# A message-passing layer on one core: fewer PSUM banks for the gather tiles, hand-written orders on four engines, and the next pair's products moved between the tiles

## The chip, the core and the metric

The kernel runs on one core of a Trainium2 chip. A core has five engines that run side by side and wait for each other by semaphores: TensorE (PE; its weight loads are PEld in the profile), VectorE (DVE), ScalarE (ACT), GpSimd (POOL) and SyncE (SP, which here only loads registers and issues transfers). [...] The metric is the device time of one execution in microseconds. Three runs of the kernel before gave 5231.43, 5231.67 and 5264.13, with a median of 5231.67.

## The reference

There are 12500 nodes with 32 features and 400000 edges, sorted by their destination. Every edge takes the normalised features of its source and its destination and 32 features of its own through two small layers. Every node takes the maximum over the edges that end in it.

```python
h = jnp.maximum(_layernorm(x, axis=-1), 0.0)
e_feat = jnp.concatenate([h[src], h[dst], edge_attr], axis=-1)   # 96 features
hid = jax.nn.relu(e_feat @ W1 + b1)                              # 64
v = hid @ W2 + b2                                                # 32
x_cand = jax.ops.segment_max(v, dst, num_segments=num_nodes)
out = x + jnp.maximum(x_cand, h)
```

## The kernel before, in words

The edges are cut into four stripes (`NS`), which lie side by side on the partitions, 32 features each. Every stripe is worked through in 196 chunks (`NCH`) of 512 edges, so that a chunk holds 2048 edges. The main loop takes two chunks, a pair, per turn: 98 turns. The first layer is split in three products that are added up in the PSUM tiles `ph0` to `ph3`, one for each stripe:

- the edge's own features: weights `w1c`, moving data `ea`, a plain transfer;
- the destination: since edges are sorted, a stripe's chunk ends in a window (span) of at most 32 nodes. The window's rows of a table `q` are the weights (`qw`), and a one-hot `of` (which node of the window an edge ends in) is the moving data. DVE makes `of` by comparing the destination numbers `db` with the node numbers `node` (line 370);
- the source: rows of `h` gathered by GpSimd with indirect DMAs of 128 rows (`gather`, line 143), turned into features by edges with a DVE transpose (`to_features`, lines 324 and 326).

Most chunks have 16 groups of 128 source rows. GpSimd gathers 12 of them, and TensorE fetches the last four (`MM`) by matmul, which the code calls tiles: a one-hot `hot` of the group of 14 nodes, in seven parts and two halves of `h` (14 matmuls, line 295), picks all features of the group, a matmul with `its` (line 292) puts a large negative number on the 13 wrong nodes, and DVE's maximum over the 14 (line 297) leaves the right row in `gm`. `hot` and `its` are made by DVE (lines 285 and 287). A pair has eight such tiles. They prepare the pair that follows; the four tiles of a chunk are taken by `next(tiles, None)` at given places of the loop.

After ACT's relu (`hid`, line 389) the second layer goes to `pv` (line 399). A DVE scan (line 404) runs the maximum along the edges, starting again at every new destination by the penalties `pb`. `leave_1` transposes the scan's result by TensorE (line 336) and adds the bias (`so`, line 338); DVE makes a one-hot `last` of the edges that are the last of their node (line 340). `leave_2` multiplies the two (line 350), ACT copies the result (`wo`, line 353), and SP writes the four windows to DRAM (line 357).

PSUM is used as follows: `ph0` to `ph3` one bank each, `pv` three buffers that tiles and second layers take in turn, `tr` one for both `leave` steps. The buffers of gathered rows are six, so the gathers of a pair can start when the transposes of the pair three turns ahead have read theirs; they are 24 in a row.

The order on SP and PE is that of the program (`manual_schedule(engines={SP, PE})`). On DVE and ACT a scheduler sets it: it puts the two transposes of line 324 for the next pair right after the product that reads the present pair's `ht`. So in DVE's stream they stand one pair ahead of their place in the program.

## Time and profile before

| | |
|---|---|
| median of 3 runs | 5231.67 us |
| profiled execution | 5227.3 us |
| its span | 5225.5 us |
| mean granted TensorE clock | 0.810 |
| PE busy | 3638.2 us (70%) |
| DVE busy | 1846.3 us (35%) |
| POOL busy | 2238.9 us (43%) |
| ACT busy | 315.6 us (6%) |
| HBM traffic | 48 GB/s over the span |

The profile is that of one execution. A row of its groups gives the line, the engine, the operation, what it writes and reads, and how often; then the busy time and the mean duration of one in ns; then how long the engine stood idle just before such instructions and what ended the wait ("issue": nothing that the profile shows; "remote": a signal whose sender had long ended). In the slices, each digit is a fortieth of the span in tenths. In a timeline, a row is a start, a time, an engine, a line and an operation, with how many were merged (x14), and in brackets how long the engine was idle before it. The first 163 us prepare tables; the loop over pairs takes the rest, but for the last some 25 us.

### The profile page before, as it was taken

What the parts mean: (1) busy time and instruction counts of PE and PEld (TensorE: products, weight loads), DVE (VectorE), ACT (ScalarE), POOL (GpSimd) and SP (SyncE); (2) the same over time, 40 slices, a digit from 0 to 9 for tenths busy, and PEclk for the clock granted to TensorE, in tenths of its full rate; (3) what the DMA queues carried; (4) which work ended last, traced back from release to release, by engine and by line L of the source; (5) the groups of instructions that cost most, each with busy time, mean ns of one, the idle gap of its engine ahead of it and who ended that gap; (6) DMA issues with size and microseconds to landing.
All of it is one profiled execution on the core that took longest, in us unless ns stands there. A gap on an engine that the chain in (4) does not pass through costs nothing. (4 is left out here: it accounts for less than half of the span.)

```text
span 5225.5 us, 57318 instructions
## 1 busy us (share of the span) xinstructions
PE 3638.2 (70%) x20281; PEld 2775.9 (53%) x20281; DVE 1846.3 (35%) x3612; ACT 315.6 (6%) x627; POOL 2238.9 (43%) x2369
## 2 busy tenths in 40 slices
PE   2376767676767676767676767676767676777687
PEld 1255555555555555555554555555555555555565
DVE  2333333333333333333333333333333333333344
ACT  1000000000000000000000000000000000000000
POOL 6534344444444444444444444444444444444420
PEclk6587878787878787878788888787878787878788
DMA  3321112211211121112111211121112211211121
GB/s 123 90 58 43 42 39 58 44 41 40 58 42 41 40 56 44 40 40 56 44 40 40 57 44 40 40 56 44 41 40 57 44 41 40 57 44 40 40 53 65
DMA packets 235577, 256.47 MB, mean 49 GB/s; under 512 B 123653, under 2 KB 211861, under 8 KB 222102
## 3 DMA queue, kind: packets, MB, share of 16 engines
q10 hardware_dynamic: 74084, 137.60, 9.7%
q0 software_dynamic: 75296, 38.70, 5.6%
q1 hardware_dynamic: 85906, 76.48, 4.9%
q8 instruction: 159, 2.61, 0.2%
q14 instruction: 132, 1.08, 0.1%
HBM read 238.44 MB, written 14.04 MB: 48 GB/s over the span
## 5 line engine op out<-in xcount | busy, mean ns | idle before, releaser
L143 POOL DMA_INDIRECT gh<-h_d,src_i x2353 | 2234.8, 950 | 2812.1 <-DVE ht L324 2098.3
L295 PE MATMUL pv<-hs,hot 128*128 128x448 f32 x10808 | 2874.0, 413 | 712.6 <-issue 712.4
L295 PEld LDWEIGHTS pv<-hs,hot 128*128 128x128 f32 x10808 | 2282.8, 212 | 1444.9 <-issue 1270.9
L297 DVE TENSOR_REDUCE gm<-pv 128x32 f32<-128x448 f32 x772 | 481.2, 623 | 2548.3 <-remote 1529.4
L292 PE MATMUL pv<-others,its 128*128 128x448 bf16 x772 | 301.9, 391 | 427.0 <-issue 386.0
L285 DVE TENSOR_SCALAR hot<-kb,key_p 128x512 fp32r<-128x512 f16 x1351 | 555.8, 479 | 9.5 <-DMA qw<-q_d 9.5
L350 PE MATMUL tr<-so,last 128*128 128x128 f32 x1568 | 250.2, 282 | 250.0 <-issue 240.8
L404 DVE TENSOR_TENSOR_SCAN sm<-pb,sm,pv 128x512 f32<-128x512 bf16 x195 | 248.9, 1276 | 469.3 <-remote 332.5
L350 PEld LDWEIGHTS tr<-so,last 128*128 128x128 f32 x1568 | 227.1, 197 | 229.5 <-issue 211.8
L389 ACT ACTIVATE hid<-ph,wt 128x512 f32<-128x512 f32 x392 | 239.3, 690 | 973.5 <-PE ph L379 529.9
L292 PEld LDWEIGHTS <-its 128*128 128x128 bf16 x772 | 78.0, 101 | 400.5 <-issue 387.4
L353 ACT ACTIVATE wo<-tr 128x128 f32<-128x128 f32 x196 | 54.5, 278 | 3810.7 <-remote 1817.6
L336 PE MATMUL tr<-ident,sm 128*128 128x128 f32 x784 | 146.0, 319 | 22.3 <-ACT wo L353 22.3
L336 PEld LDWEIGHTS tr<-ident,sm 128*128 128x128 f32 x784 | 117.9, 167 | 57.9 <-ACT wo L353 38.4
L338 DVE TENSOR_TENSOR so<-tr,wt 128x512 f32<-128x512 f32 x196 | 133.9, 683 | 24.1 <-PE pv L292 11.5
L340 DVE TENSOR_TENSOR last<-iota_w,at 128x512 f32<-128x512 f32 x196 | 131.6, 672 | 28.2 <-PE tr L350 28.2
L324 DVE STREAM_TRANSPOSE ht<-gh 128x384 f32<-128x384 f32 (+1 forms) x196 | 102.9, 563 | 71.0 <-PE ph L379 54.8
L379 PE MATMUL ph<-ea,wt 32*64 32x512 f32 x1568 | 110.0, 617 | 8.4 <-DMA ea<-in_edge_attr 8.4
L379 PE MATMUL ph<-ht,wt 32*64 32x512 f32 x1568 | 110.9, 612 | 0.5 <-issue 0.4
L379 PE MATMUL ph<-of,qw 32*64 32x512 f32 x1568 | 105.5, 592 | 6.2 <-issue 6.2
L399 PE MATMUL pv<-hid,wt 64*32 64x512 f32 x1568 | 108.9, 604 | 0.2 <-ACT hid L389 0.2
L287 DVE TENSOR_SCALAR its<-kb,place 128x512 bf16<-128x512 f16 x193 | 69.6, 361 | 96.4 <-remote 80.1
(68 smaller groups left out, 399.3 us busy)
## 6 DMA issues: line engine op xcount, KB each, us to landing
ea<-in_edge_attr SPq DMA_DIRECT2D x49, 1024.0 KB
db<-in_dst_ext ACTq DMA_DIRECT2D x196, 256.0 KB
kb<-key_d ACTq DMA_DIRECT2D x193, 256.0 KB
gh<-h_d,src_i POOLq DMA_INDIRECT x2353
pb<-pen_d ACTq DMA_DIRECT2D x196, 128.0 KB
qw<-q_d SPq DMA_DIRECT2D x784, 8.0 KB
top_d<-wo SPq DMA_DIRECT2D x784, 4.0 KB
top_d<-zero ACTq DMA_DIRECT2D x2, 1568.0 KB
```

Source lines behind the costliest of these rows:

```text
L143: nc.gpsimd.indirect_dma_start(out=gh[:, k, :], out_offset=None, in_=h_d[:, :], in_offset=bass.IndirectOffsetOnAxis(ap=src_i[:, c, k:k + 1 ...
L285: nc.vector.tensor_scalar(hot[:, k], kb[:, 0], key_p[:, k:k + 1], None, op0=ALU.is_equal)
L292: nc.tensor.matmul(po, its[:, e], others.rearrange("p f a -> p (f a)"), start=True, stop=False)
L295: nc.tensor.matmul(po, hot[:, k, e], hs[:, part, k].rearrange("p f a -> p (f a)"), start=False, stop=(k == A1 - 1 and part == 1))
L297: nc.vector.tensor_reduce(gm[:, m, :], po.rearrange("p (f a) -> p f a", a=A0), axis=AX.X, op=ALU.max)
L336: nc.tensor.transpose(px[:, j, :], sm[:, j * P:(j + 1) * P], ident)
L338: nc.vector.tensor_tensor(so, px, b2r[:, None, :].to_broadcast([P, J, P]), op=ALU.add)
L340: nc.vector.tensor_tensor(last, iota_w[:, None, None, :].to_broadcast([P, J, NS, W]), at[:, :, c * J:(c + 1) * J].rearrange("p s j -> p j ...
L350: nc.tensor.matmul(pw, last[:, j].rearrange("p s w -> p (s w)"), so[:, j, :], start=(j == 0), stop=(j == J - 1))
L379: nc.tensor.matmul(ph[s][x * HID:(x + 1) * HID], w[g], e[g], start=start, stop=stop)
L389: nc.scalar.activation(hid[s], ph[s], AF.Relu, bias=b1c)
L404: nc.vector.tensor_tensor_scan(sm, loaded.pop(c + x)[2], pv[x], before, op0=ALU.add, op1=ALU.max)
```

## The change

- **PSUM.** `pv` has two buffers instead of three. The free bank holds `iota_ps`, a copy of the constants 0 to 31 that `last` is compared with; before, they were read from SBUF.
- **One-hots of node spans.** ACT makes `of` with two activations: relu(1 - (db - node)^2). The constants are kept with the other sign (`below`).
- **Orders.** DVE and ACT are in program order too. Each turn of the loop names the place of every operation. The transposes are done at the start of the pair that needs them.
- **Interleaving.** The products of the next pair's edge features and windows into `ph` are done in this turn, after the third tile and after the second layer. The window sums of a pair's second chunk (`leave_2`) are done in the turn that follows.
- **Window sums.** `leave_2` computes two blocks of 64 by 64 instead of one of 128 by 128, of which it had read only the diagonal; ACT copies half the columns.
- **Loads.** `AHEAD` is 4 chunks instead of 2; `db` and `pb` are one transfer each for all stripes; `kb` is loaded for two chunks at once; SP loads the window starts for a pair at once, from a transposed table, without bounds checks; `qw` has eight buffers, `sm` and `of` three.

```diff
-AHEAD = 2
+AHEAD = 4
...
-            tc.manual_schedule(engines={SP, PE}):
+            tc.manual_schedule(engines={SP, PE, DVE, ACT}):
...
+        iota_ps = ps.tile([P, C], F32, name="iota_ps")[:, :W]
+        nc.vector.tensor_copy(iota_ps, iota_w)
...
+        def tile(c, m):
...
+            hot, its = hots[c]
+            e = slice(m * P, (m + 1) * P)
+            po = ps.tile([P, C], F32, name="pv", bufs=2)[:, :D * A0]
+            nc.tensor.matmul(po, its[:, e], others.rearrange("p f a -> p (f a)"), start=True, stop=False)
+            for k in range(A1):
+                for part in range(2):
+                    nc.tensor.matmul(po, hot[:, k, e], hs[:, part, k].rearrange("p f a -> p (f a)"),
+                                     start=False, stop=(k == A1 - 1 and part == 1))
+            rows = mm_rows[c][:, m, :]
+            nc.vector.tensor_reduce(rows, po.rearrange("p (f a) -> p f a", a=A0), axis=AX.X, op=ALU.max)
...
-                for s in range(NS):
-                    g = slice(s * D, (s + 1) * D)
-                    nc.scalar.dma_start(db[g, :n], ap(dst_ext, 1 + s * S + c * C, [[0, D], [1, n]]))
-                    nc.scalar.dma_start(pb[g, :n], ap(pen_d, s * S + c * C, [[0, D], [1, n]]))
+                nc.scalar.dma_start(db[:, :n], ap(dst_ext, 1 + c * C, [[S, NS], [0, D], [1, n]]))
+                nc.scalar.dma_start(pb[:, :n], ap(pen_d, c * C, [[S, NS], [0, D], [1, n]]))
...
+        def window_hots(c):
+
+            of = ofs[c] = pool.tile([P, C], F32, name="of", bufs=3)
+            nc.scalar.activation(of, loaded[c][1], AF.Square, bias=below[:, c:c + 1])
+            nc.scalar.activation(of, of, AF.Relu, bias=ones, scale=-1.0)
...
-                nc.tensor.matmul(pw, last[:, j].rearrange("p s w -> p (s w)"), so[:, j, :],
-                                 start=(j == 0), stop=(j == J - 1))
+                for g in range(2):
+                    nc.tensor.matmul(pw[g * 2 * W:(g + 1) * 2 * W],
+                                     last[:, j, 2 * g:2 * g + 2].rearrange("p s w -> p (s w)"),
+                                     so[:, j, g * 2 * D:(g + 1) * 2 * D], start=(j == 0), stop=(j == J - 1))
...
+            a, b = c + 2, c + 3
+            gh = [gather(c + x) for x in range(2)]
+            load_keys(a + 2)
             for k in range(c + AHEAD, min(c + AHEAD + 2, NCH)):
                 load(k)
...
             ht = [to_features(c + x, gh[x]) for x in range(2)]
-            into_ph([(w1a, ht[x]) for x in range(2)], False, True)
+            into_ph(ph, [(w1a, ht[x]) for x in range(2)], False, True)
             hid = []
             for s in range(NS):
                 hid.append(pool.tile([P, C], F32, name="hid", bufs=6))
                 nc.scalar.activation(hid[s], ph[s], AF.Relu, bias=b1c)
...
+            for k in range(a, min(a + 2, NCH)):
+                window_hots(k)
+            tile(a, 0)
+            one_hots(b, range(3))
+            tile(a, 1)
+            one_hots(b, range(3, A1))
+            last = [lasts(c)]
+            tile(a, 2)
+            ph = edges_into(a)
+            pv = [ps.tile([P, C], F32, name="pv", bufs=2) for x in range(2)]
             for s in range(NS):
                 for x in range(2):
                     g = slice(x * HID, (x + 1) * HID)
                     nc.tensor.matmul(pv[x][s * D:(s + 1) * D], w2x[g], hid[s][g], start=True, stop=True)
+            windows_into(a, ph)
+            leave()
             sms = []
...
+            tile(a, 3)
+            so = leave_1(c, sms[0])
+            last.append(lasts(c + 1))
+            tile(b, 0)
+            one_hots(a + 2, range(4))
+            leave_2(c, so, last[0])
+            tile(b, 1)
+            so = leave_1(c + 1, sms[1])
+            one_hots(a + 2, range(4, A1))
+            tile(b, 2)
+            tile(b, 3)
+            leave = lambda c=c + 1, so=so, last=last[1]: leave_2(c, so, last)
+        leave()
```

In the order that follows from it, TensorE's turn is: the product of `ht`; tiles a0, a1, a2; the edges' product of the next pair; the second layer; the windows' product of the next pair; the window sums of the last turn's second chunk; tile a3; transposes of the first chunk; tile b0; window sums of the first chunk; tile b1; transposes of the second chunk; tiles b2 and b3. DVE's turn is: four transposes (rows of the gathers and of the tiles, by turns); the maxima of a0 and a1 with one-hots between them; `last`; the maximum of a2; two scans; the maximum of a3; and so on to the maxima of b2 and b3.

## The prediction

> **What bounds the kernel.** I read the page's slices first, then its groups, then stretches with and without gathers, then one pair in order of time. A pair is two chunks, one turn of the loop.

> ```profile
> PE   2376767676767676767676767676767676777687
> PEclk6587878787878787878788888787878787878788
> ...
> L143 POOL DMA_INDIRECT gh<-h_d,src_i x2353 | 2234.8, 950 | 2812.1 <-DVE ht L324 2098.3
> ...
> L297 DVE TENSOR_REDUCE gm<-pv 128x32 f32<-128x448 f32 x772 | 481.2, 623 | 2548.3 <-remote 1529.4
> ...
> L353 ACT ACTIVATE wo<-tr 128x128 f32<-128x128 f32 x196 | 54.5, 278 | 3810.7 <-remote 1817.6
> ```

> TensorE is busy some 70% of every slice, at a granted clock of about 0.8. DVE and ACT stand idle for "remote": the awaited signal came, but nothing that had just ended explains the moment.

> ```profile
> 2502.50:2555.30 52.80, 37.88 (x213) 28.96 (x213) 20.22 (x41) 2.98 (x6) 22.71 (x24) 0.82 0.10 20
> ...
> 5073.35:5104.75 31.40, 31.40 (x210) 25.55 (x210) 18.22 (x37) 3.23 (x7) 0.00 (x0) 1.00 0.18 42
> ```

> The columns are the stretch, its length, busy us (instructions) of PE, PEld, DVE, ACT and POOL, clock, DMA share, GB/s. The second row is a pair at the end, when all gathers are issued: TensorE is never idle, at full clock, and the pair takes 31.2 us. With 24 gathers in it the same pair takes 52.8 (from gather burst to burst 52.2 on average). So a burst of gathers costs 21 us a pair. The timeline shows how:

> ```profile
> 2521.50 0.95 POOL L143 DMA_INDIRECT gh<-h_d,src_i  x1 [23.02 <-DVE ht L324]
> ...
> 2527.01 1.09 PE L399 MATMUL pv<-hid,wt 64*32 64x512 f32 x16
> ...
> 2528.07 3.13 PE L295 MATMUL pv<-hs,hot 128*128 128x448 f32 x14
> ...
> 2531.50 1.28 DVE L404 TENSOR_TENSOR_SCAN sm<-pb,sm,pv 128x512 f32<-128x512 bf16 x1 [3.60 <-PE pv L295]
> ...
> 2533.62 0.35 DVE L287 TENSOR_SCALAR its<-kb,place 128x512 bf16<-128x512 f16 x1 [0.84 <-remote]
> ...
> 2544.13 0.53 PE L295 MATMUL pv<-hs,hot 128*128 128x448 f32 x1 [1.57 <-issue]
> 2546.23 0.53 PE L295 MATMUL pv<-hs,hot 128*128 128x448 f32 x1 [1.57 <-issue]
> ...
> 2550.28 0.95 POOL L143 DMA_INDIRECT gh<-h_d,src_i  x1 [0.30 <-issue]
> ...
> 2553.24 0.62 DVE L297 TENSOR_REDUCE gm<-pv 128x32 f32<-128x448 f32 x1 [18.08 <-remote]
> ...
> 2555.33 0.91 PE L295 MATMUL pv<-hs,hot 128*128 128x448 f32 x2 [0.87 <-issue]
> ```

> Call the first gather G (2521.50). The product that the scan needs ends at 2528.1; the scan starts at 2531.50. The tile begun at 2528.04 is computed by 2531.2, but its maximum starts at 2553.24. Between the signal for `its` (a tile's first weights) and that for the tile's end lie 28 TensorE instructions (14 weight loads, 14 matmuls): 19.6 us, 0.70 each. So in a burst TensorE's completions reach the others one per 0.70 us, small matmul or large. The scan's signal is roughly the 81st instruction after G and comes at G+10.0, so some 66 pass freely (81 - 10.0/0.70). TensorE runs about 65 instructions ahead of what has been told, then crawls itself, 0.70 or 1.40 apart. It ends at G+33.8 (2555.33), 5 us after the last gather's start. I know no cause, only the pace; DVE and ACT instructions that don't wait for TensorE run promptly.

> **The change, part by part.** TensorE's work, from this timeline: a tile 3.01 us (30 instructions), each of three groups into `ph` 1.05 (32), the second layer 1.03 (32), transposes of a chunk 0.52 (8), window sums 0.97 (16). 8 x 3.01 + 3 x 1.05 + 1.03 + 2 x 0.52 + 2 x 0.97 = 31.2, the pair without gathers. Before, 17.0 of that lies between the end of the slow stretch and the next G (2502.5 to 2521.5, which took 19.0: the clock was at half at first, so 1.9 is lost), and 14.2 is done in the 33.8 us from G.

> *Hand order of DVE.* The transposes of gathered rows, which release the next burst, stood a pair ahead in DVE's stream; now they stand after the maximum of the pair's last tile, and TensorE's next instruction after that tile is the product that reads them. Nothing covers this: 0.1 signal + 0.62 maximum + four transposes (rows 563 and 304 ns, about 1.6 as they overlap) + 0.1 = 2.4 us of idle TensorE a pair. G falls after the first, 1.6 after the tile, 0.85 before the product. Below zero is excluded: before, no such wait stands in the trace.

> *TensorE order with two tile banks.* From G: product of `ht` (32 instructions), tiles a0, a1, a2 (90), products of the next pair's edges (32), then the second layer into both banks that a1 and a2 hold. It waits for DVE's maximum of a2, and that for a2's end, instruction 122 after G. At one per 0.70 us it is told at (122 - 66) x 0.70 = 39 us, later than the stretch's end; so at G+33.8 all is told, the maximum takes 0.62 and the second layer starts at G+34.6. Until then TensorE has done 1.05 + 9.03 + 1.05 = 11.1 us of work, not 14.2. Behind the waiting matmul are queued the window products, the previous chunk's window sums (for which ACT's copy, then SP's writes wait) and tile a3; behind DVE's waiting maximum, both scans.

> [...] By the rows 3.01 against 0.62 two banks do outside the burst: cost 0. [...]

> *One-hots of node spans on ACT.* Two fewer DVE operations (482 ns), four more activations (690 ns), 2.8 us. They run under a0 to a2 (9 us) and are needed after the second layer. DVE has 18 us of work in 52. Cost 0; uncovered it would be 2.8 on TensorE.

> *Constants in PSUM.* `last` costs 672 ns; the PSUM-reading `so` 683: nothing. [...] By the row it is 0: POOL's idle time before a gather is 0.30 with DVE busy or not, and in the worst stretch DVE did nothing for 18 us. I take 0.

> *Window sums.* Eight products 64x64 for four 128x128, so 32 instructions for 16. Nearest row 0.11 us per weight load; between 0.5 (halves side by side) and 1.8 (every instruction at the old price); I take 0.9, as half the columns load per instruction. They stand after the stretch. Ends: -80 and +175 us over 196.

> *Loads.* ACT issues two `db`/`pb` transfers for eight, one `kb` for two; SP reads registers once a pair, without bounds steps; loads run a pair further ahead, past SP's writes. These queues wait for `wo` most of the time (3382.9 us on SP); cost 0, hidden by a pair's lead (over 50 us).

> Sum of a pair: 33.8 + 0.8 + (31.1 - 11.1 = 20.0) + 1.9 half clock + 1.6 to the next G = 58.1, against 52.2: +5.9. About 94 pairs carry a burst, four don't (+2.4 each): 555 + 10 = +565 on the profiled execution's 5227.3 (span 5225.5), which is 0.1% under the median of 5231.67. Forecast 5795.

> **The rivals.**
> *The second layer gets in early* (chance 0.10). If the free 66 instructions are more (packed groups may count less), a2 is told inside the stretch, and the layer, window products and sums start there: about 13.7 us of work in the burst, pair 56, 5590. For: their matmuls start 7 ns apart. Against: the second layer before was packed too and its signal was late.
> *A burst costs 21 us wherever it falls* (0.10). Then the order does nothing and only the 2.4 us are added: 5227 + 98 x 2.4 = 5460. For: a burst always has 24 gathers. Against: the pace counts instructions, so contents matter.
> *The slow stretch shortens* (0.11, faster). Place: the stretch's end. If its length is set by what the change thins (DVE's SBUF reads, ACT's and SP's DMA issues), each us less is worth 94 us; from 6 us of 27 it beats the kernel before. A third shorter (9 us): pair 49.1, 4950. Against: gathers keep their 1.25 us beat with all these engines standing still.
> *Within 1%* (0.03): two misses that cancel.
> The forecast keeps 0.66: its own range 5690 to 5950, from the window sums' ends and 0.5 us a pair either way in the half clock.

> **Numbers.** Range 5450 to 5950: the forecast and the first two rivals, 0.86. Under 1% this measurement tells nothing. Faster 0.11, same 0.03, slower 0.86.

> **What will show it.** After: bursts some 58 us apart; in each, TensorE silent or crawling from about G+13 to G+34 with the second layer starting just after; the maximum of the third tile idle for "remote" 15 to 20 us; some 2.4 us of TensorE idle before each `ht` product; end pairs without gathers of 33.6 us. The prediction is wrong if the second layer starts well inside the burst, or if DVE's signals from TensorE come promptly there.

## The result, and the profile after

The changed kernel took 5621.14 us (median of four executions, 5611.26 to 5643.38) where the kernel before took 5238.3 (5231.43 to 5264.13): a ratio of 1.073, interval 1.067 to 1.078. It is slower by 7%, inside the predicted range of 5450 to 5950 and 174 us under the predicted 5795; the forecast's own range, 5690 to 5950, was missed. The profiled execution took 5611.26 us, its span 5609.5, at a mean granted clock of 0.797.

From the profile's page of the changed kernel, the slices and a group (busy us and mean ns, then the idle time ahead and what ended it):

```profile
PE   2666676777676666667676777676767676757676
PEclk6777878787878787878787878787878787878788
...
L144 POOL DMA_INDIRECT gh<-h_d,src_i x2353 | 2273.5, 966 | 3204.9 <-DVE ht L358 2458.6 <-issue 683.1 <-DVE ht L356 29.2
```

TensorE is busy for 67% of the span, where it was 70%, and GpSimd waits longer for DVE before its bursts (2458.6 us, before 2098.3). TensorE's groups tell where its new idle time stands. First two of them before:

```profile
L379 PE MATMUL ph<-ht,wt 32*64 32x512 f32 x1568 | 110.9, 612 | 0.5 <-issue 0.4
...
L399 PE MATMUL pv<-hid,wt 64*32 64x512 f32 x1568 | 108.9, 604 | 0.2 <-ACT hid L389 0.2
```

and after:

```profile
L400 PE MATMUL ph<-of,qw 32*64 32x512 f32 x1568 | 422.6, 1047 | 121.3 <-issue 119.3
L449 PE MATMUL pv<-hid,wt 64*32 64x512 f32 x1568 | 294.9, 986 | 1414.8 <-DVE gm L323 785.6 <-issue 627.4 <-ACT hid L435 0.7
...
L400 PE MATMUL ph<-ht,wt 32*64 32x512 f32 x1568 | 180.0, 641 | 135.9 <-DVE ht L358 135.9
```

The second layer (L449) is what stands in the slow stretch: 1415 us ahead of it, where it was 0.2. The product of the rows `ht` now waits 135.9 us in all for DVE, 1.4 us a pair, where it was 0.5 in all.

One pair from the timeline (start, duration, engine, line and operation; in brackets the idle time before it):

```profile
2702.66 1.76 PE L400 MATMUL ph<-ht,wt 32*64 32x512 f32 x16 [1.40 <-DVE ht L358]
2702.68 0.94 POOL L144 DMA_INDIRECT gh<-h_d,src_i  x1 [25.56 <-DVE ht L358]
...
2714.05 0.62 DVE L323 TENSOR_REDUCE gm<-pv 128x32 f32<-128x448 f32 x1 [4.39 <-PE pv L320]
2715.00 0.61 PE L449 MATMUL pv<-hid,wt 64*32 64x512 f32 x1
...
2726.00 0.62 DVE L323 TENSOR_REDUCE gm<-pv 128x32 f32<-128x448 f32 x1 [8.88 <-remote]
...
2726.68 1.96 PE L449 MATMUL pv<-hid,wt 64*32 64x512 f32 x14 [9.96 <-issue]
...
2738.48 1.12 PE L386 MATMUL tr<-so,last 128*64 128x64 f32 x16
2739.59 4.75 PE L320 MATMUL pv<-hs,hot 128*128 128x448 f32 x14
...
2759.45 1.76 PE L400 MATMUL ph<-ht,wt 32*64 32x512 f32 x16 [1.40 <-DVE ht L358]
```

The burst starts at G = 2702.68. TensorE runs the product, three tiles and the edge products without a stop. Two matmuls of the second layer enter when tile a1's maximum is through (2715.00). The other 14 wait for the maximum of tile a2. DVE is told of that tile's end, and starts on it, at 2726.00: G+23.3 here, G+28.6 in the median of 80 bursts. The window products follow, crawling, and at 2738.48 TensorE is free again. The first tile after that takes 4.75 us instead of 3.1, at half clock. A pair ends, as it began, with 1.40 us of nothing.

Stretches of the same profile (length, busy us and instructions of PE, PEld, DVE, ACT, POOL, granted clock, DMA share, GB/s):

```profile
2714.00:2738.50 24.50, 11.26 (x50) 1.98 (x36) 5.36 (x10) 0.00 (x0) 14.54 (x15) 0.60 0.07 11
2738.50:2759.48 20.98, 19.58 (x120) 17.13 (x116) 9.60 (x20) 0.45 (x2) 0.00 (x1) 0.89 0.24 53
5509.36:5543.92 34.56, 33.16 (x224) 25.72 (x224) 17.29 (x36) 5.55 (x10) 0.00 (x0) 0.95 0.01 2
```

The first row is the rest of the slow stretch: TensorE does 11.3 us of work in 24.5, DVE and ACT are nearly idle. The second is what is left for after it, at a clock of 0.89. The last row is a pair without a gather. It took 31.2 us before and takes 34.56 now: the new order costs time without any burst too.

Over the middle 80 bursts the median pair is 56.3 us, against 52.2 before. On average over them TensorE is free of the stretch at G+36.2 (before G+34.4), and what follows up to the next G takes 20.1 us (before 17.8). So each part of the pair gave about 2 us. As a sum over the profiled executions: 93 pairs between the third product of the rows and the third-last took 51.66 us each before and 56.22 after, +424; what lies ahead of them became 49 us shorter, what lies behind 9 longer; +384, as the two spans differ.

### The profile page after: what moved, and what is told of

It reads as the page before. It is cut to its first block, busy times and chain, and to the rows that moved or that the text cites. A ratio compares the mean times of both kernels' runs of the same rounds, so it can differ in the third digit from the quotient of the medians.

```text
span 5609.5 us, 58146 instructions
## 1 busy us (share of the span) xinstructions
PE 3764.3 (67%) x21849; PEld 2580.9 (46%) x21849; DVE 1767.2 (32%) x3417; ACT 565.7 (10%) x1019; POOL 2277.6 (41%) x2369
## 5 line engine op out<-in xcount | busy, mean ns | idle before, releaser
L144 POOL DMA_INDIRECT gh<-h_d,src_i x2353 | 2273.5, 966 | 3204.9 <-DVE ht L358 2458.6
L320 PE MATMUL pv<-hs,hot 128*128 128x448 f32 x10808 | 2503.3, 387 | 1.1 <-issue 1.0
L320 PEld LDWEIGHTS pv<-hs,hot 128*128 128x128 f32 x10808 | 2116.2, 196 | 165.7 <-issue 2.6
L449 PE MATMUL pv<-hid,wt 64*32 64x512 f32 x1568 | 294.9, 986 | 1414.8 <-DVE gm L323 785.6
L449 PEld LDWEIGHTS pv<-hid,wt 64*32 64x32 f32 x1568 | 35.9, 132 | 1587.2 <-DVE gm L323 853.6
L400 PE MATMUL ph<-of,qw 32*64 32x512 f32 x1568 | 422.6, 1047 | 121.3 <-issue 119.3
L400 PEld LDWEIGHTS ph<-of,qw 32*64 32x64 f32 x1568 | 86.5, 192 | 463.0 <-issue 460.7
L400 PE MATMUL ph<-ht,wt 32*64 32x512 f32 x1568 | 180.0, 641 | 135.9 <-DVE ht L358 135.9
L386 PEld LDWEIGHTS tr<-so,last 128*64 128x64 f32 x3136 | 139.4, 172 | 191.3 <-issue 186.2
L386 PE MATMUL tr<-so,last 128*64 128x64 f32 x3136 | 171.0, 266 | 9.0 <-issue 6.4
L350 ACT ACTIVATE of<-db,below 128x512 f32<-128x512 int32 x196 | 141.8, 724 | 64.1 <-DMA db<-in_dst_ext 64.1
L351 ACT ACTIVATE of<-of,ones 128x512 f32<-128x512 f32 x196 | 142.0, 724 | 6.4
```

Source lines behind the costliest of these rows:

```text
L144: nc.gpsimd.indirect_dma_start(out=gh[:, k, :], out_offset=None, in_=h_d[:, :], in_offset=bass.IndirectOffsetOnAxis(ap=src_i[:, c, k:k + 1 ...
L320: nc.tensor.matmul(po, hot[:, k, e], hs[:, part, k].rearrange("p f a -> p (f a)"), start=False, stop=(k == A1 - 1 and part == 1))
L350: nc.scalar.activation(of, loaded[c][1], AF.Square, bias=below[:, c:c + 1])
L351: nc.scalar.activation(of, of, AF.Relu, bias=ones, scale=-1.0)
L386: nc.tensor.matmul(pw[g * 2 * W:(g + 1) * 2 * W], last[:, j, 2 * g:2 * g + 2].rearrange("p s w -> p (s w)"), so[:, j, g * 2 * D:(g + 1) * ...
L400: nc.tensor.matmul(ph[s][x * HID:(x + 1) * HID], w[g], e[g], start=start, stop=stop)
```

## The experiments

Theory A: the change costs by its order alone, through the gap of TensorE ahead of the product of the rows and the half-clock tile behind it. Rival B: the second layer held up by two shared tile banks. Apart from them stands the question what a burst does to either order.

The experiments came with a surprise that has to be told first. They ran in four groups, each on another chip, and on each of these the kernel before took 3192 to 3194 us, not 5235: gathers ran just as densely (983 ns each on average in the changed kernel and 1006 in the one before with narrow sums, 0.30 us apart; in the first comparison 966 in the changed kernel and 950 in the one before), but TensorE's completions were told promptly: in the changed kernel's timeline below a tile ends at 1530.24 and its maximum starts at 1530.28, while in the timeline above tile a2 had ended at 2713.61 when its maximum started at 2726.00. The cost of the late completions could therefore not be tested, and of each expectation below only the part for prompt completions. What could be tested is what the change costs there: 281 us, against 383 in the first comparison.

### No gathers: plain transfers in their place

```diff
-        for k in range(K - MM * (c in MMC)):
-            if c * C + k * D < SE:
-                nc.gpsimd.indirect_dma_start(out=gh[:, k, :], ...)
+        n = min(K - MM * (c in MMC), (SE - c * C) // D)
+        nc.sync.dma_start(gh[:, :n], h_v[:, :n])
```

The loads are issued two (before) or four chunks (after) ahead. Both kernels then work on wrong source rows, so these times leave the gathering out.

> The kernel before with its 2353 indirect gathers left out: GpSimd issues nothing in the loop, and SP fetches as many consecutive rows of h with one plain transfer per chunk, so the values are other rows' than the reference's. My theory, that a burst of gathers slows what TensorE can tell the others: every pair takes what the gather-free pairs at the end took, 31.2 us, so about 3240 us in all, granted clock near 1. Rival, that TensorE's clock or the waits in the order are what costs 21 us a pair: it stays above 4800 us.

> The same in the changed kernel: no indirect gathers, plain transfers of other rows. It shows what the new order costs by itself. My theory: 2.4 us of TensorE idle before each product of ht and, as in its gather-free pairs at the end (34.6 us), a slower clock after it: 3480 to 3570 us, 240 to 330 over e1. Rival, that the whole loss is made inside the bursts: the same as e1 within 50 us.

The kernel before without gathers took 3423.47 us (one execution), longer than with them on the same chip (3194.39); the expectation of 3240 missed. A group of TensorE, and one of DVE's waits (us in all, times, longest):

```profile
L398 PE MATMUL pv<-hid,wt 64*32 64x512 f32 x1568 | 181.8, 665 | 124.0 <-DVE gm L295 123.5 <-ACT hid L388 0.2
...
DVE ht L323 <- DMA gh<-h_d: 783.7, 196, 8.6
```

DVE's transposes wait for the plain transfers, which land late: 783.7 us in all. The tile maxima stand behind them in DVE's order, and the second layer waits for these, 123.5 us, up to 4.3 at a time. So this run is not a clean control for the gathers. It hints that short gaps of TensorE cost more than their length (124 us of idle time, 229 us longer, at a clock of 0.967), in a kernel that has nothing else of the change.

The changed kernel without gathers took 3480.94 us (one execution): within its own expected 3480 to 3570, but only 57 us over the other, not the expected 240 to 330, since the other was too slow. With gathers it took 3473.41 on another chip (below): where completions are prompt, its gathers cost nothing that shows.

### The window sums alone

```diff
-                nc.tensor.matmul(pw, last[:, j].rearrange("p s w -> p (s w)"), so[:, j, :], ...)
+                for g in range(2):
+                    nc.tensor.matmul(pw[g * 2 * W:(g + 1) * 2 * W], last[:, j, 2 * g:2 * g + 2]...,
+                                     so[:, j, g * 2 * D:(g + 1) * 2 * D], ...)
```

First put into the kernel before; then taken back in the changed kernel.

> One part of the change alone, put into the kernel before: window sums as eight 64x64 products instead of four 128x128. There one of a pair's two window sums lies inside the burst. My theory, that a burst lets through a number of TensorE instructions whatever their size: 16 more in the burst push out 16 instructions of a tile (1.6 us), against 0.35 us saved on each sum outside: about +1 us a pair, 5330 us (5290 to 5370). Rival, that work and not instructions counts: 0.7 us a pair less, 5170 us.

> The same edit undone in the changed kernel, where both sums stand behind the slow stretch. My theory: each costs 0.35 us more again and no instruction is missing in the burst: +0.7 us a pair, 5690 us. Rival, that fewer instructions are worth something everywhere: 5560 us or less.

In the kernel before: 3208.54 us, ratio 1.0042 (1.0029 to 1.0056). In the changed kernel with the old sums: 3480.41, ratio 1.0893 (1.0876 to 1.091), as the changed kernel itself (below). The 16 narrow products take 0.62 us on the timeline up to the next start, the old ones 0.89, but neither kernel got faster by it. In the first one, 64 of 93 pairs take 30.7 us, 0.5 less than the 31.2 of before, but the others take 31.2 to 36.3, so the mean is 31.4. Its gathers set that:

```profile
L143 POOL DMA_INDIRECT gh<-h_d,src_i x2353 | 2366.3, 1006 | 741.9 <-issue 655.9 <-DMA gh<-h_d,src_i 46.0 <-DMA h_d<-h 25.0
...
DVE ht L324 <- DMA gh<-h_d,src_i: 356.8, 92, 10.6
```

GpSimd makes no pause between bursts: 24 gathers of 1.006 us, each with 0.30 ahead of it, are 31.3 us, the mean pair. DVE's transposes wait for the rows, 356.8 us in all; tile maxima stand behind them, and at times the second layer waits for a maximum, 34.8 us in all. Less work for TensorE does not help there. (Of the kernel before itself no trace with prompt completions was kept.) Why the changed kernel gained nothing either, the clock shows further below.

### The changed kernel itself, and its gap undone in three ways

All of this group ran on one chip.

> The changed kernel itself, so that the next three have it beside them on the same chip. Two cases, told apart by the kernel before on the same chip. If the kernel before takes about 5235 us there (TensorE's completions are told late while rows are gathered), it takes about 5620 again. If the kernel before takes about 3194 us, as on the chip of the four runs before these (no such lateness), theory A (what the change costs is its order alone: TensorE stands still 1.87 us ahead of the product of the rows, and the tile behind it runs at half clock in four pairs of ten) gives 98 pairs x (34.1 - 31.3) us more: about 3465, 3440 to 3495. Rival B (the cost is the two shared tile banks under a late second layer) gives 3194 to 3250 there, since nothing is late.

The changed kernel took 3473.41 us, ratio 1.0883 (1.0865 to 1.0901). Theory A's 3465 is met; rival B's 3194 to 3250 is not. The gap on this chip, from its timeline:

```profile
1528.28 1.96 PE L320 MATMUL pv<-hs,hot 128*128 128x448 f32 x9
1530.28 0.62 DVE L323 TENSOR_REDUCE gm<-pv 128x32 f32<-128x448 f32 x1 [2.39 <-PE pv L320]
1530.82 0.57 DVE L356 STREAM_TRANSPOSE ht<-gh 128x384 f32<-128x384 f32 x1
1531.31 0.27 DVE L358 STREAM_TRANSPOSE ht<-gm 128x128 f32<-128x128 f32 x1
1531.50 0.54 DVE L356 STREAM_TRANSPOSE ht<-gh 128x384 f32<-128x384 f32 x1
1531.63 2.05 PE L400 MATMUL ph<-ht,wt 32*64 32x512 f32 x16 [1.40 <-DVE ht L358]
1531.96 0.27 DVE L358 STREAM_TRANSPOSE ht<-gm 128x128 f32<-128x128 f32 x1
...
1533.66 4.42 PE L320 MATMUL pv<-hs,hot 128*128 128x448 f32 x14
```

The last tile ends at 1530.2; then come the maximum and, one after the other, four transposes. The product starts after the second and stops again for the fourth, so it takes 2.05 us instead of 1.1. The clock goes down behind it:

```profile
1530.23:1531.63 1.40, 0.01 (x1) 0.00 (x0) 1.35 (x4) 0.00 (x0) 0.00 (x0) 1.00 0.09 18
1531.63:1533.61 1.98, 1.98 (x16) 0.42 (x16) 0.60 (x2) 0.00 (x0) 1.65 (x2) 0.84 0.10 12
1533.61:1538.10 4.49, 4.49 (x22) 3.89 (x17) 0.00 (x0) 4.40 (x8) 3.27 (x5) 0.69 0.10 11
1538.10:1541.30 3.20, 3.20 (x17) 2.84 (x17) 1.98 (x5) 0.69 (x1) 2.59 (x3) 1.00 0.11 15
```

The granted clock is 0.84 in the product and 0.69 in the tile behind it (4.49 us instead of 3.1), and full again in the next. Of 93 pairs, 67 have this and take 34.5 us; 26 haven't and take 32.9. A gap of 1.40 us, with about 0.65 us of stops in the product behind it, was enough for it in 7 pairs of 10.

Which pairs are hit is no chance. In the traces the granted clock changes only at points 3.41 us apart (in the two of the first comparison all 304 and 244 of its records begin within 0.04 us of such a point, and give full clock or half). Here are the intervals between such points around this gap, which begins at 1530.23, and around the one two pairs later, which begins at 1599.29:

```profile
1529.58:1532.99 3.41, 2.02 (x20) 0.69 (x18) 1.96 (x5) 0.00 (x0) 1.03 (x2) 1.00 0.06 12
1532.99:1536.40 3.41, 3.41 (x15) 2.49 (x9) 0.00 (x0) 2.77 (x5) 2.74 (x3) 0.50 0.14 14
...
1597.84:1601.25 3.41, 2.02 (x10) 1.17 (x8) 1.92 (x5) 0.00 (x0) 0.54 (x1) 1.00 0.07 14
1601.25:1604.67 3.42, 3.42 (x28) 2.34 (x27) 0.04 (x1) 2.22 (x4) 2.51 (x4) 1.00 0.09 14
```

The first stop, 1.40 and 0.65 us, lies whole in one interval, and the next interval runs at half clock. The second begins 1.45 us into its interval and reaches into the next; the clock stays full. In all 67 pairs that were hit the gap began 0.12 to 1.32 us into its interval; of the 26 others, 25 began later and one at 0.41. With the old sums it is 39 pairs at 0.63 to 1.27 and 54 at 1.32 to 2.24. This closes the sum: 2.05 us of stop and 67/93 of 1.6 us of half clock are 3.2 us a pair, 315 us in all.

It also explains why small savings vanished. A pair of 34.5 us is 0.4 longer than ten intervals (34.13), one of 32.9 is 1.2 shorter, so the gap wanders through its interval and the mean pair stays at ten intervals: 34.09 us here, 34.12 with the old sums, 34.11 without gathers. What the narrow sums gave, the clock took.

The first way to undo it leaves DVE's order to the planner:

```diff
-            tc.manual_schedule(engines={SP, PE, DVE, ACT}):
+            tc.manual_schedule(engines={SP, PE, ACT}):
```

> One part of the change undone: VectorE's order is the planner's again (TensorE's, ScalarE's and SyncE's stay written by hand). The transposes of the gathered rows then lie a pair ahead, and behind the last tile maximum of a pair there are only the transposes of the tile rows. Theory A: the wait ahead of the product of the rows falls from 1.87 us to 0.7 to 1.0, and the half-clock tile behind it mostly goes: 1.0 to 1.8 us a pair less than the changed kernel, 100 to 175 us in all (about 3330 beside 3465, or about 5480 beside 5620). Rival B: VectorE has time to spare, so nothing moves: within 20 us of the changed kernel.

3306.93 us, ratio 1.0361 (1.0343 to 1.0378): 166 us less than the changed kernel, inside theory A's 100 to 175.

```profile
L400 PE MATMUL ph<-ht,wt 32*64 32x512 f32 x1568 | 213.9, 617 | 38.8 <-DVE ht L358 38.7
```

The row gives 38.8 us of idle time ahead of the product's instructions, where it was 136.0. That is less than the whole stop: two matmuls now enter early and the rest stand behind them, so the product takes some 1.5 us longer than undisturbed. The expected 0.7 to 1.0 was too little. All pairs but one (32.9) take 32.2 to 32.5 us: no half-clock tile is left.

The second fills the gap with work that the change had taken away from there:

```diff
             windows_into(a, ph)
-            leave()
...
-            leave = lambda c=c + 1, so=so, last=last[1]: leave_2(c, so, last)
-        leave()
+            leave_2(c + 1, so, last[1])
```

> The changed kernel with the window sums of a pair's second chunk put back to the pair's end, ahead of the product of the rows, in place of behind the next pair's window products. Nothing is taken away: 16 products of 0.69 us move into TensorE's gap. Theory A: the gap of 1.87 us falls to 1.1 to 1.2, and with a gap so short the half-clock tile goes in part: 0.7 to 1.4 us a pair less, 65 to 135 us in all (about 3365 beside 3465, or about 5520 beside 5620). Rival B, and any theory by which the sums are what costs: no gain, within 20 us.

3353.05 us, ratio 1.0507 (1.049 to 1.0525): 120 us less, inside theory A's 65 to 135, although nothing was taken away.

```profile
L400 PE MATMUL ph<-ht,wt 32*64 32x512 f32 x1568 | 174.7, 617 | 75.3 <-DVE ht L358 75.3
```

0.77 us of gap a pair remain, less than the expected 1.1 to 1.2, and the product still stops for 0.65. No pair has the half-clock tile: all 93 take 32.7 to 33.0 us. So a stop of 2.05 us took the clock down when it lay in one interval, and stops of 1.4 to 1.5 us, in these two runs, never did.

The third does the filling and puts the transposes of the gathered rows a pair ahead, by hand:

```diff
-            gh = [gather(c + x) for x in range(2)]
...
+            for x in range(2):
+                rows_in(a + x)
...
-            leave()
...
+            leave_2(c + 1, so, last[1])
```

`rows_in` issues a chunk's gathers and transposes its rows.

> Both in one, VectorE's order still by hand: the transposes of the gathered rows are put a pair ahead, right behind the product of the rows, and the window sums lie in what is left of the gap. Theory A: the gap closes to 0.1 to 0.4 us and the half-clock tile goes: 2.0 to 2.6 us a pair less, 195 to 255 us in all (about 3235 beside 3465; about 5395 beside 5620). Rival B: within 20 us of the changed kernel. If the kernel before is late here (5235 us) and this one still comes out over 5450, the burst adds a cost of its own with the shared banks.

3263.55 us, ratio 1.0218 (1.0201 to 1.0235): 210 us less, as expected. Two waits of TensorE remain, both small:

```profile
L318 PE MATMUL pv<-others,its 128*128 128x448 bf16 x772 | 276.8, 359 | 37.6 <-DVE sm L466 36.9 <-issue 0.8
...
L409 PE MATMUL ph<-ht,wt 32*64 32x512 f32 x1568 | 130.9, 622 | 30.6 <-DVE ht L367 30.6
```

The first is a trace of the two shared banks: with the sums moved away from behind the window products, tile a3 comes to its bank before the scan has read it, 0.54 us a pair on the timeline. The second way, which moves the sums too, has the same wait, 36.2 us in all.

### One tile ahead of the product; and the third bank

```diff
             ht = [to_features(c + x, gh[x]) for x in range(2)]
+            tile(a, 0)
             into_ph(ph, [(w1a, ht[x]) for x in range(2)], False, True)
...
-            tile(a, 0)
             one_hots(b, range(3))
```

> The changed kernel with one call moved: the first tile of the next chunk is computed ahead of the product of the rows, in place of behind it, so that TensorE has 3.1 us of other work while VectorE takes the last maximum and makes the four transposes (1.87 us of gap). All the rest of the change stays: two tile banks, one-hots on ScalarE, narrow sums, VectorE's order by hand. Theory A: the gap goes whole, and with it the half-clock tile and the product stretched by waits; a pair comes to 30.7 to 31.2 us, as the best pairs of the kernel before with narrow sums (30.7). On a chip where the kernel before takes about 3192: 3145 to 3200, 275 to 325 us less than the changed kernel, and the same as the kernel before or up to 1.5% faster. Where the kernel before takes about 5235: 3.0 to 3.5 us a pair less than the changed kernel, 5290 to 5340. Rival B (the tile banks, or anything but the gap): 3440 or more, 5550 or more.

3157.91 us, ratio 0.9888 (0.9872 to 0.9905): with one line moved, the changed kernel is 9% faster than it was and 1.1% faster than the kernel before.

```profile
1523.48 0.57 DVE L356 STREAM_TRANSPOSE ht<-gh 128x384 f32<-128x384 f32 x1
1523.76 2.22 PE L320 MATMUL pv<-hs,hot 128*128 128x448 f32 x10
1523.97 0.27 DVE L358 STREAM_TRANSPOSE ht<-gm 128x128 f32<-128x128 f32 x1
1524.17 0.54 DVE L356 STREAM_TRANSPOSE ht<-gh 128x384 f32<-128x384 f32 x1
1524.63 0.27 DVE L358 STREAM_TRANSPOSE ht<-gm 128x128 f32<-128x128 f32 x1
1525.91 1.11 PE L400 MATMUL ph<-ht,wt 32*64 32x512 f32 x16
```

The same four transposes lie under the tile (its last ten matmuls are the second row), and are done 1 us before the product. TensorE waits 1.5 us for them in the whole execution, where it was 136.0, and all pairs take 30.86 us. GpSimd's gathers say that there is little more to gain:

```profile
L144 POOL DMA_INDIRECT gh<-h_d,src_i x2353 | 2312.8, 983 | 755.3 <-issue 661.4 <-DMA gh<-h_d,src_i 53.0 <-DMA h_d<-h 24.7
```

GpSimd never waits for DVE any more. Its gathers stand end to end: 983 ns and 0.30 of issue, so 24 of them take 30.8 us, as long as a pair.

The third bank was put back alone:

```diff
-        iota_ps = ps.tile([P, C], F32, name="iota_ps")[:, :W]
-        nc.vector.tensor_copy(iota_ps, iota_w)
...
-            po = ps.tile([P, C], F32, name="pv", bufs=2)[:, :D * A0]
+            po = ps.tile([P, C], F32, name="pv", bufs=3)[:, :D * A0]
```

> One part of the change undone: tiles and second layer have three PSUM banks again, and the counter for the one-hots of last edges is read from SBUF again; orders as changed. Theory A: where the kernel before takes about 3192 us it gives nothing, within 15 us of 3473, since the second layer never waits for a bank there; VectorE reading both operands of 392 one-hots from SBUF may hold up GpSimd's issue but not the end. Where the kernel before takes about 5235 us the second layer waits for one maximum less in the stretch and comes 12 us earlier in it, but the stretch lets only one told completion pass per 0.70 us either way: 5560 to 5630. Rival B (the shared banks are what costs): 3250 to 3300, or 5380 to 5480.

3467.39 us, ratio 1.0855 (1.0837 to 1.0873), where the changed kernel had 1.0883 (1.0865 to 1.0901) in its own group: nothing that can be told from no change. Again 67 pairs take 34.5 us and 26 take 32.9. Where completions are prompt, the banks and the counter in PSUM neither cost nor save time in this order. Rival B is out there.

### Where the 1.1% come from

The kernel with the tile ahead, once with DVE's order left to the planner (the edit of the first way above), once with three banks.

> The kernel with the tile ahead of the product of the rows, and VectorE's order left to the planner (the other three orders by hand). It tells where the 1.1% comes from by which that kernel was faster than the kernel before. Theory A2: from VectorE's order by hand, since the kernel before with narrow sums had half of its pairs at 30.7 us and the others at up to 35.5, and this one had all at 30.86: with the planner's order back, single pairs stall again and the mean pair rises by 0.3 to 0.7 us, 3185 to 3230 where the kernel before takes about 3192. Rival B2: from what the change takes off VectorE and TensorE (one-hots on ScalarE, narrow sums, paired loads): stays at 3150 to 3170. Where the kernel before takes about 5235: 5290 to 5400 by either, less than the changed kernel's 5621, since the gap is gone.

> The kernel with the tile ahead of the product of the rows, and with three PSUM banks for tiles and second layer, the counter read from SBUF. Where the kernel before takes about 3192 us: within 10 us of 3158, nothing waits for a bank. Where it takes about 5235: the second layer waits for an earlier maximum and its 16 products enter earlier; theory A 5270 to 5340, and by the rival that the shared banks cost in the stretch this one alone gets down to 5200 to 5250.

With the planner's order 3174.72 us, ratio 0.9951 (0.9935 to 0.9968), between the two theories' numbers; with three banks 3165.46, ratio 0.991 (0.9893 to 0.9926), no difference, and again all pairs at 30.86 us. With the planner's order most pairs take 30.9 us too, but some up to 31.9, one 32.2 and one 32.9; DVE's transposes wait for gathers there, 232.8 us in all. So the order by hand gives 0.3% (beside the kernel with three banks, on the same chip) to 0.6% of the 1.1.

The runs do not separate the rest. An estimate points to the gathers: they took 1006 ns on average in the kernel before with narrow sums and 983 ns here, and 24 x 0.023 = 0.55 us is what the mean pairs differ by (31.43 and 30.86). How long gathers take beside DVE's work stands in the next section, under the constants.

## Why the prediction was right, and where its sum was off

The direction and the main thought, that orders and not operations decide, hold. The number was in part luck: 5621 lies in the range of 5450 to 5950 because that took in the first two rivals. The sum for a pair with a burst was 58.1 us and 56.3 was measured. By its steps:

- **Hand order of DVE: 2.4 us.** The wait is where it was put. It is 1.40 us ahead of the product, and about 0.65 more in which the product stops for the second chunk's transposes: 2.05. What the step missed is the clock. In the pair without gathers the next tile ran at half clock, so that pair took 34.56 us, not 33.6. With prompt completions this part alone is the whole cost: undoing it by one moved tile gave 315 us.
- **Two tile banks: the second layer at G+34.6.** This is the step that failed. The prediction called itself wrong if the second layer started well inside the burst, and it does: the first two products entered at G+12.3 and the others, in the median burst, at G+29.3. The term that was mis-sized is the number of instructions that pass freely. With 0.70 us each behind it, the maximum of a1 (instruction 92, told at G+11.4) and that of a2 (122, at G+28.6) give 76 and 81, not 66. Nor is it one number: over 80 bursts a2 was told at G+15 to G+34, and in 14 of them only at G+33.8, as the sum had it for all. So the rival by which the second layer gets in early was the right one for this step: its pair was 56, its time 5590. Second layer and window products came into the stretch, and only 17.3 us of work were left behind it, not 20.0. In return the stretch lasted to G+36.2 on average, and not to G+33.8 with 0.8 of waiting. Whether a third bank makes the pair shorter where completions are late was not tried.
- **One-hots on ACT, loads: 0.** Right for TensorE. In the changed kernel on the later chip, products with `of` waited 17.6 us for ACT in the whole execution, the start included.
- **Constants in PSUM: 0 by the row.** For the time, 0 fits what was measured: taking the counter back to SBUF moved nothing (3467 beside 3473 us). But the row that was read, the idle time ahead of a gather, shows only a part. It is 0.30 us after as before; what is longer beside some of DVE's operations is the gather itself:

```profile
518.76 1.06 POOL L144 DMA_INDIRECT gh<-h_d,src_i  x1 [0.31 <-issue]
518.91 0.68 DVE L366 TENSOR_TENSOR last<-iota_ps,at 128x512 f32<-128x512 f32 x1
...
486.21 1.65 POOL L144 DMA_INDIRECT gh<-h_d,src_i  x1 [0.30 <-issue]
486.35 0.69 DVE L364 TENSOR_TENSOR last<-iota_w,at 128x512 f32<-128x512 f32 x1
```

  The first two rows are the changed kernel on the later chip, the others the same with the counter in SBUF; in both, `its` ends just after the gather's start. In these two traces a gather beside an idle DVE, or beside maxima, scans and transposes, takes 944 ns. Beside `last` alone it takes 944 too in the changed kernel, and 21 of 154 take over 1000 with the counter in SBUF; beside `its` and `last` 1051 and 1599 on average. Beside `hot` alone it takes 1032 in either. In the first comparison the changed kernel's gathers took 946 ns beside an idle DVE and beside `last` alone, 1052 beside `its` and `last`, 1035 beside `hot`. Why, no run shows. The longer gathers cost no time in these two kernels, where GpSimd still waits about 300 us in all for DVE before its bursts (324.5 in the changed kernel).
- **Window sums: 0.9.** They take 0.69, or 0.62 up to the next start; right in kind, and worth nothing in the end.
- **Half clock of 1.9 behind the stretch, 1.6 up to the next G.** The tile behind the stretch lost 1.6. The tail is there.

So the 5795 were too high by 174 us. Too much work was put behind the stretch (2.7 us a pair) and a little too much half clock and waiting (0.7); the later end of the stretch (1.6) gave part of that back.

The rival by which a burst costs 21 us wherever it falls gave 5460, 160 too little. Its 2.4 us for the order were near the 2.05 measured, and the half clock does not fill what is missing: it came behind the gap in only 23 of the 93 pairs of the first comparison, and these took 56.1 us, the others 56.2. About 2 us of the 4.1 that a pair with a burst lost are therefore made in the stretch: a burst is no fixed cost.

The two rivals that would have ended at no change or faster did not come: the slow stretch became longer, not shorter.

What stays open: why completions were late in the first comparison and not in the other four (it is not known on which chip the first ran, so chip and hour cannot be told apart); what the later end of the stretch comes from, which no run tested; and whether the kernel with the tile ahead beats the kernel before where completions are late. An estimate from the numbers above: without the 2.05 us of stop a pair is 54.2, still over the 52.2 of before, since the stretch ends later.

## What to carry to other kernels

When an order is written by hand, look at each place where one engine's result goes through a second engine and back, and put a piece of the first engine's other work in between that is longer than the round trip. Here a tile of 3.1 us over a chain that stopped TensorE for 2.05 us turned 9% slower into 1% faster, with no instruction added or taken away. Price such a gap at more than its length: a stop of 2.05 us took the clock down behind it in 67 of 93 pairs, and stops of 1.4 to 1.5 us never did, so half filling it was worth more than the filling. And when a saving does not show, look whether the pair's length has been caught by something else, here by the clock's intervals or by the gathers.

## What the runs showed of the hardware

The same kernel took 5231 us in the first comparison and 3192 to 3194 on four chips in the others, with gathers at nearly the same pace (950 ns on average there, 1006 ns in its sister with narrow sums, in both 0.30 us apart). The late completions that make up 2000 us of the first number are therefore no property of gathers as such. In the first comparison they begin a number of instructions behind the start of a burst, some 76 to 81 in the median burst of the changed kernel, and then come at one per 0.70 us (28 instructions in 19.6 us in the kernel before). On another chip, in the kernel with the tile ahead, gathers ran without a break (983 ns each, 0.30 us apart) under a TensorE that had no stop in the loop's pairs, all of 30.86 us.

In the changed kernel on the later chip, and in the same with the counter in SBUF, gathers took 944 ns beside an idle DVE, and longer beside some of its one-hots: 1032 ns on average beside `hot`, and beside `its` and `last` together 1599 where `last` read its counter from SBUF, 1051 where from PSUM. In the first comparison the changed kernel's took 946 beside an idle DVE, 1035 beside `hot`, and 1052 beside `its` and `last`. No run shows by what way.
